# A two-layer graph transformer kernel: layer 0's unranked token tile becomes a block of its own, and the keys, list scatters and readback come in another order

## The chip, the cores and the metric

The kernel runs on one core of one Trainium2 chip. The metric is the device time of one execution in microseconds (us). Three runs of the kernel before took 1982.24, 1981.65 and 1976.04 us; their median is 1981.65 us. One more execution was profiled: it took 1979.62 us, of which 1977.7 us lie between its first and last instruction (the span). Unless another one is named, every time below is a time of that execution, counted from the start of its span.

## The reference

2708 tokens of width 512 pass through two layers of the same form. `adj` is a symmetric 0/1 matrix with ones on its diagonal; its rows are sparse (the longest has 20 entries). Cut to what matters, one layer is

```python
mask = adj.astype(float32) + eye(n)
q = (h @ Wq.T + bq).reshape(n, 8, 64)      # k and v likewise
scores = einsum('nhd,mhd->hnm', q, k) / sqrt(64)
scores = where(mask == 0, -1e9, scores)
attn = softmax(scores, axis=-1)
ctx = einsum('hnm,mhd->nhd', attn, v).reshape(n, 512)
h1 = layer_norm(h + ctx @ Wo.T + bo, ln1_g, ln1_b)
ff = relu(h1 @ W1.T + b1) @ W2.T + b2      # 512 -> 2048 -> 512
h2 = layer_norm(h1 + ff, ln2_g, ln2_b)
```

All of it is float32.

## The kernel before, in words

Work is tiled by 128 tokens: 21 full tiles and one of 20 tokens, 22 in all. Attention goes over the edges only. Each token has a list of its neighbours; the keys and values of a neighbour stand in one row of 1024 numbers of a table in HBM (`kv_d`), and an indirect DMA on POOL's queue (`gather`, L1063 on, recorded as L1065) fetches, for 128 tokens at once, one neighbour each (0.5 MB).

**Groups.** So that few gathers are wasted, tokens are sorted by the length of their lists into groups of 128. Group g has the static cap `CAPS[g]`: groups 0 to 19 fall from 22 to 5, group 20 (`FRESH`) has 18, the short group 21 has 3. Group FRESH isn't sorted: it is one token tile as it stands, number `STAR`, 18 before. Its lists are at hand as soon as the lists of all tiles are made; those of the other groups must first be scattered to their ranks in HBM (`rec_d`, 21 indirect DMAs, L800) and read back into the tile `new` (three DMAs, L814 and L822).

**Keys stage** (`first`). For each token tile PE projects k and v (8 matmuls of 128x512 each), DVE adds the bias to k (L908), ACT copies v (L911), and ACT's queue writes the rows to `kv_d`. Beside it `lists(t)` makes the lists: SP loads 1.35 MB of `adj` into one of two buffers (L679), POOL adds the diagonal (L680), ACT turns the row into codes (L684), DVE takes the largest of 11 segments (L687) and of those (L691, L694). `LEAD` = 1.3 lists are started for each key tile. The first key tiles were 20 and 21 (128 and 20 tokens, one block `XBS - 1` of x), then 0 to 19; x is loaded by SP in blocks of 256 columns, each behind lists already asked for. A tile of at most 32 tokens is projected in four quarters of the array (L571), and DVE adds three quarters afterwards (`plus_rest`, L586 for k and v).

**Query stage** (`first_queries`). PE projects q for the 22 tiles in the order of `tiles`, number j by j; DVE scales and adds the bias (L962, L973) and SP writes pairs of tiles to `q_d`. The first is STAR's. Between the tiles stand the steps of attention: `next(ahead)` and `advance(c)` go on with the generator `attend`, which asks for gathers some chunks ahead and computes one chunk (two slots of a list, `SLOTS` = 2) per step: `weights` (DVE, L1101 and L1107), one step later `weigh` (ACT exponentials and half of the products, L1120 and L1127; DVE the rest, L1133 and L1140), then `sums` (DVE, last L1163) and `divided` (ACT, tile `cx`, L1171). `moving` steps through `ranked`: 8 scatters at j = 2, two per j for j = 3 to 8, and at j = 9 the last one and the readback. `own_rows` fetches the x rows of the second group (19) at j = 11, `listed` turns the readback into indices at j = 17 and 18, `own_query` projects group 19's q at j = 19. At the last j `through(0)` runs attention until both groups of block 0 are done, and `attended` follows for each: PE turns cx (tp, L1255), projects with Wo (o, L576), DVE and POOL normalise (L1239 to L1249, POOL's L1245).

**Blocks.** The feed-forward part goes over blocks of two groups, w = 256 columns: for each of 16 slices f PE makes four matmuls pf (128x256, L1446), ACT applies bias and relu (ft, L1457), and three slices later PE adds one matmul of 128x512 for each group (a, L1419). Each logical f32 matmul is two records in the trace. Layer 0 has 11 blocks: (20, 19), (18, 17), (7, 9), ..., (21, 8). During block k, `through(k + 1)` at f = 10 (f = 11 in block 0) runs attention until the groups of the next block are done; the next slice projects them with Wo; at the last slice they are turned (`turned`). The keys and values of layer 1 of block k are made in block k + 1, f = 5 to 8. Between, each f steps attention by `PACE` (0.62 chunks in layer 0).

**What sets the order.** PE, ACT and SP run in the order of the program text. POOL does so until the end of block 0; DVE does in the query stage and until slice f = 5 of block 0 (`by_turns`), and elsewhere its order is a scheduler's. [...]

Of the kernel before, what the change touches and what calls it, by code (L numbers as in the profile page):

```python
# [18 lines left out]
P = 128  # L19
# [15 lines left out]
Q4 = 32  # L35

CAPS = (22, 14, 13, 12, 12, 11, 11, 10, 10, 9, 9, 9, 9, 8, 8, 8, 7, 7, 6, 5, 18, 3)
FRESH, STAR = 20, 18
SLOTS = 2
QB = 3  # L40
LAG = 3
# [3 lines left out]
XB, XBS = 256, 11  # L45
# [427 lines left out]
def by_edges(ctx: ExitStack, tc: tile.TileContext, x, xT, adj, layers, out, good):  # L473
# [9 lines left out]
    nc = tc.nc  # L483
# [366 lines left out]
    def first(w, meanwhile):  # L850

        nonlocal at
        xg = []
        stream = [XBS - 1] + list(range(XBS - 1))
        homes = [f"w{1 + i % 2}_{i // 2}" for i in range(XBS)]
        homes = homes[1:] + homes[:1]

        def load():
            i = len(xg)
# [34 lines left out]
        counts = counted()  # L894
        done, before = 0, None
        by_turns = ExitStack()
        for i, t in enumerate([NT - 2, NT - 1] + list(range(NT - 2))):
            r = size(t)
            if i == NT - 2:
                by_turns.enter_context(tc.manual_schedule(engines={mybir.EngineType.DVE}))  # L900
                next(counts)
            xs = tokens(t)
            home = ("w2_5", "w2_6", "w2_7", "w1_6", "w1_7")[i % 5]
            kv = wts.tile([P, 2 * DM], F32, tag=home, name="kvs")
            k = project(xs, r, wk, "k")
            if i == 0:
                finish(turning)
            nc.vector.tensor_tensor(kv[:r, :DM], k[:r], bk[:r], ALU.add)  # L908
            plus_rest(kv[:r, :DM], k, r)
            v = project(xs, r, wv, "v", other=True)  # L910
            nc.scalar.copy(kv[:r, DM:], v[:r])  # L911
            plus_rest(kv[:r, DM:], v, r)
            if before:
                nc.scalar.dma_start(**before)
            before = dict(out=kv_d[0][t * P : t * P + r, :], in_=kv[:r])
            if i == 0:
                finish(load())
                finish(load())
            while done < min(NT, 1 + LEAD * i):
                lists(done)  # L920
# [14 lines left out]
    def first_queries(bq, wq, counts, ranked, listed, tables, tokens, meanwhile):  # L935
# [15 lines left out]
            return own[g]  # L951

        moving = None
        tiles = [STAR] + [t for b in range(STAR // 2, NT // 2) for t in (2 * b, 2 * b + 1)]
        tiles = [t for i, t in enumerate(tiles) if i == 0 or t != STAR]
        tiles += range(STAR // 2 * 2)
        for j, t in enumerate(tiles):
            r = size(t)
            q = project(tokens(t), r, wq, "q", other=j % 2 > 0)
            if j == 0:  # L960
                to = new_q(FRESH)
                nc.vector.scalar_tensor_tensor(to, q, DK**-0.5, bq, ALU.mult, ALU.add)  # L962
                nc.sync.dma_start(out=q_d[0][t * P : (t + 1) * P, :], in_=to)
                next(ahead)
            else:
                if not made or len(made[-1][0]) == 2:
# [6 lines left out]
                nc.vector.scalar_tensor_tensor(  # L973
                    qs[:r, i], q[:r], DK**-0.5, bq[:r], ALU.mult, ALU.add
                )
                plus_rest(qs[:r, i], q, r, DK**-0.5)
            if j == 2:
                moving = ranked(*counts)
                for _ in range(8):
                    next(moving)  # L980
            if j > 2:
                advance(0.75)
                if j < 9:
                    for _ in range(2):
                        next(moving, None)
                elif above is None:
                    finish(moving)
                    tables.__exit__(None, None, None)
                    above = ctx.enter_context(
                        tc.tile_pool(name="above", bufs=1, side="right", reuse_waits="tile")  # L990
                    )
            if j == 11:
                xr = own_rows(order[1])
            if j == 17:
                listed(True)
                all_listed.append(True)
                advance(1.5)
            if j == 18:
                listed(False)
# [529 lines left out]
    NB = len(blocks)  # L1529
    orders = [[g for block in blocks for g in block] for blocks in plans]  # L1530
    blocks, order = plans[0], orders[0]

    def attend(n, got):
# [6 lines left out]
        for g in order:  # L1540
            cuts = chunks_of(g)
            steps += [(g, s0, c, i, i + 1 == len(cuts)) for i, (_, s0, c) in enumerate(cuts)]
            if g == order[1] or (n == 0 and g == order[0]):
                steps += [None] * 3
            if n == 0 and g == order[0]:
                steps.append("more")
# [71 lines left out]
    def beside_queries(j):  # L1618
# [14 lines left out]
    def both(a, b):  # L1633
        hs = []
        for part in (a, b):
            *_, h = part
            hs += h
        yield hs

    def temp():  # L1640
        return dn.tile([P, DM], F32, tag="h", name="temp", bufs=4)
# [6 lines left out]
    early[0] = list(early[0])  # L1648
    behind, pool = None, []
    for n in range(NL):  # L1650
        blocks, order = plans[n], orders[n]
        last = n == NL - 1
        nxt = None if last else Layer(n + 1, layers[n + 1])
        if n > 0:
# [24 lines left out]
        for k, block in enumerate(blocks):  # L1679
# [4 lines left out]
            for f, zs in enumerate(now.feed_forward(block, hs, hT)):  # L1684
                if f == NFC:
                    break
                if f == 5:
                    by_turns.close()
                if f in (5, 6, 7, 8) and behind:
                    next(behind)  # L1690
# [4 lines left out]
                if more and f == 11 + (k + n == 0):  # L1695
# [122 lines left out]
```

## Time and profile before

| what | us |
|---|---|
| median of three runs | 1981.65 |
| the profiled execution | 1979.62 |
| its span | 1977.7 |
| PE busy | 1858.0 |
| DVE busy | 1363.1 |
| ACT busy | 960.4 |
| POOL busy | 829.6 |

The span's 40 slices, with the busy share in tenths, show where PE isn't filled: mostly in the first eight slices (49.4 us each), which hold the keys, the queries and block 0. The prediction shows the lines. In the timelines each row is: start, duration, engine, line, operation, output<-inputs, shapes, count, and in brackets the idle time before it with what ended it. A count of 8 pf records is one slice f.

### The profile page before, as it was taken

The numbers are of one execution on the slowest core, as the hardware profiler recorded it, in microseconds if no ns is written. First come the engines' busy times: TensorE is split into PE (matmuls) and PEld (weight loads), VectorE is DVE, ScalarE is ACT, GpSimd is POOL, SyncE is SP. The second block draws the span as 40 slices with busy tenths as digits, with TensorE's granted clock in tenths as the row PEclk, the third lists the DMA queues.
The fourth block names the chain that finished last, engine by engine and source line by source line (L and its number), as shares of the span: only waits on it lengthen the run. The fifth ranks groups of instructions, "written<-read, shape, count | busy, mean of one in ns | idle before, by whom it ended". The sixth has DMA issues, their size and how long they took to land. (4 is left out here: it accounts for less than half of the span.)

```text
span 1977.7 us, 20995 instructions
## 1 busy us (share of the span) xinstructions
PE 1858.0 (94%) x6126; PEld 1094.8 (55%) x6126; DVE 1363.1 (69%) x2215; ACT 960.4 (49%) x3334; POOL 829.6 (42%) x732
## 2 busy tenths in 40 slices
PE   9799758899999999999999997999999999999997
PEld 3344325556566555655656553565566666666664
DVE  6886558758658686684840337586977999899522
ACT  3651226455537545474442213555465766666511
POOL 3114636535536455452410114353545765557101
PEclk9899979899999999999999999999999999999998
DMA  9995658556555565563411368565664776565000
GB/s 326 353 308 197 226 207 278 207 170 202 180 176 169 207 211 176 181 193 120 163 38 64 98 241 325 188 235 170 224 207 154 259 237 228 178 214 182 25 1 19
DMA packets 128751, 372.63 MB, mean 188 GB/s; under 512 B 17340, under 2 KB 31516, under 8 KB 125918
## 3 DMA queue, kind: packets, MB, share of 16 engines
q0 software_dynamic: 72176, 257.59, 39.2%
q1 hardware_dynamic: 45940, 92.02, 13.3%
q10 hardware_dynamic: 10510, 21.58, 3.0%
q8 instruction: 50, 0.82, 0.2%
q14 instruction: 75, 0.61, 0.1%
HBM read 320.33 MB, written 50.81 MB: 188 GB/s over the span
## 5 line engine op out<-in xcount | busy, mean ns | idle before, releaser
L1065 POOL DMA_INDIRECT kv<-kv_d,idx x442 | 569.8, 1289 | 486.3 <-DVE acc L1140 243.1
L1446 PE MATMUL pf<-hT,w 128*128 128x256 f32 (+1 forms) x2816 | 637.1, 374 | 7.2 <-ACT ft L1457 4.9
L1419 PE MATMUL a<-w,ft 128*128 128x512 f32 x1312 | 622.6, 600 | 12.5 <-ACT ft L1457 10.1
L1446 PEld LDWEIGHTS pf<-hT,w 128*128 128x128 f32 x2816 | 520.8, 191 | 182.6 <-issue 102.6
L1101 DVE TENSOR_TENSOR kv<-kv,q 128x1024 f32<-128x1024 f32 (+1 forms) x232 | 268.2, 1165 | 209.7 <-DMA kv<-kv_d,idx 171.8
L1419 PEld LDWEIGHTS a<-w,ft 128*128 128x128 f32 x1312 | 249.7, 193 | 209.4 <-issue 170.2
L1457 ACT ACTIVATE ft<-pf,b 128x256 f32<-128x256 f32 (+1 forms) x336 | 153.9, 463 | 416.8 <-PE pf L1446 413.7
L1127 ACT ACTIVATE kv<-kv,p 128x64 f32<-128x64 f32 x1328 | 335.2, 334 | 5.4
L1107 DVE TENSOR_REDUCE sc<-kv 128x16 f32<-128x1024 f32 (+1 forms) x232 | 267.2, 1160 | 1.6
L1140 DVE TENSOR_TENSOR acc<-acc,kv 128x1024 f32<-128x1024 f32 (+2 forms) x188 | 217.1, 1155 | 17.1 <-ACT kv L1127 13.9
L1245 POOL TENSOR_TENSOR rd<-va,mhalf 128x1 f32<-128x1 f32 (+1 forms) x88 | 91.1, 1035 | 286.9 <-DVE va L1243 285.9
L1120 ACT ACTIVATE p<-sc,minus 128x8 f32<-128x8 f32 (+1 forms) x442 | 108.1, 294 | 137.8 <-DVE sc L1107 115.1
L576 PE MATMUL o<-wo,cT 128*128 128x512 f32 x336 | 153.7, 610 | 12.0 <-ACT cT L1260 12.0
L1133 DVE TENSOR_TENSOR kv<-kv,p 128x512 f32<-128x512 f32 (+1 forms) x188 | 128.0, 681 | 24.1 <-ACT p L1120 24.1
L1171 ACT ACTIVATE cx<-acc,su 128x64 f32<-128x64 f32 (+1 forms) x352 | 88.5, 334 | 67.3 <-DVE su L1163 37.0
L576 PEld LDWEIGHTS o<-wo,cT 128*128 128x128 f32 x336 | 65.2, 196 | 95.7 <-issue 72.9
L684 ACT ACTIVATE code<-aj 128x2708 bf16<-128x2708 int32 (+1 forms) x22 | 71.0, 3227 | 50.3 <-POOL aj L680 48.5
L687 DVE MAX8 tops<-code 128x8 f32<-128x247 f32 (+2 forms) x242 | 84.0, 399 | 14.7 <-ACT code L684 14.5
L576 PE MATMUL k<-wk,xg 128*128 128x512 f32 x168 | 79.6, 618 | 15.2 <-DVE kvs L908 10.6
L1127 ACT ACTIVATE acc<-kv,p 128x64 f32<-128x64 f32 (+1 forms) x352 | 88.8, 334 | 1.5
L1028 POOL DMA_INDIRECT kv_d<-kvs,ident_i x22 | 24.5, 1114 | 154.9 <-ACT kvs L1506 94.8
L1249 DVE SCALAR_TENSOR_TENSOR h<-h,rd,ln_b 128x512 f32<-128x512 f32 (+1 forms) x88 | 65.6, 747 | 33.8 <-POOL rd L1245 33.8
(165 smaller groups left out, 1501.2 us busy)
## 6 DMA issues: line engine op xcount, KB each, us to landing
aj<-in_adj SPq DMA_DIRECT2D x21, 1354.0 KB
kv_d<-kvs ACTq DMA_DIRECT2D x21, 512.0 KB
w<-in_W ACTq DMA_DIRECT2D x16, 512.0 KB
w<-in_W SPq DMA_DIRECT2D x16, 512.0 KB
kv<-kv_d,idx POOLq DMA_INDIRECT x442
q_d<-qs SPq DMA_DIRECT2D x23, 256.0 KB
zT_d<-zT SPq DMA_DIRECT2D x22, 256.0 KB
xb_d<-h SPq DMA_DIRECT2D x21, 256.0 KB
```

The source lines that it names most:

```text
L576: nc.tensor.matmul(o[:r], xs(c), wm[:, c, :], start=(c == 0), stop=(c == NC - 1))
L1065: return nc.gpsimd.indirect_dma_start(out=to, out_offset=None, in_=table[:, :], in_offset=bass.IndirectOffsetOnAxis(ap=s, axis=0), bounds_ ...
L1101: nc.vector.tensor_tensor(kv[:r, :c, :DM], kv[:r, :c, :DM], self.q[:r].unsqueeze(1).to_broadcast([r, c, DM]), ALU.mult,)
L1107: nc.vector.tensor_reduce(self.sc[:r, s0 : s0 + c, :], kv[:r, :c, :DM].rearrange("p s (h d) -> p s h d", d=DK), AX.X, ALU.add,)
L1120: nc.scalar.activation(p[:r, s, :], self.sc[:r, s, :], AF.Exp, bias=minus[:r, g, s : s + 1])
L1127: nc.scalar.activation(to[:, i, hd], kv[:r, i, DM + h * DK : DM + (h + 1) * DK], AF.Copy, scale=p[:r, s0 + i, h : h + 1],)
L1133: nc.vector.tensor_tensor(to[:, 0, :].rearrange("p (h d) -> p h d", d=DK), kv[:r, 0, DM:].rearrange("p (h d) -> p h d", d=DK), p[:r, s0, : ...
L1140: nc.vector.tensor_tensor(self.acc[:r, :c, :], self.acc[:r, :c, :], kv[:r, :c, DM:], ALU.add)
L1245: nc.gpsimd.tensor_tensor(rd[:r], va[:r], mhalf[:r], ALU.pow)
L1419: nc.tensor.matmul(a[:r], fts[f][:, c0 : c0 + r], self.w2[f // 2][:, f % 2, :], start=(f == 0), stop=(f == NFC - 1),)
L1446: nc.tensor.matmul(pf[:, :w], self.w1[f // 2][:, c, f % 2 * P : f % 2 * P + P], hT[:, c, :w], start=(c == 0), stop=(c == NC - 1),)
L1457: nc.scalar.activation(ft[:, :w], pf[:, :w], AF.Relu, bias=self.b1[:, f : f + 1])
```

## The change

- `STAR` is 10 instead of 18: group FRESH is token tile 10. `CAPS` stays as it is.
- Layer 0 has 12 blocks: (20) alone, (19, 18), (17, 16), (7, 9), (6, 10), (5, 11), (0, 15), (1, 14), (2, 13), (3, 12), (4) alone, (21, 8). Layer 1's plan is the same as before.
- Keys come in the order 0 to 15, 20, 21, 16 to 19, and one block of x less is loaded at the start. Queries come in the order 10, 11, 0 to 9, 12 to 21.
- The scatters go 8 at j = 2, three per j for j = 3 to 6 and one at j = 7; the readback follows at j = 12, x rows of group 19 at j = 13.
- `through(0)`, which now asks for group FRESH alone, and its `attended` come at j = 19, ahead of group 19's query; tiles 20 and 21 are projected after it. `both` and the calls at the end of the query stage are gone.
- FRESH's x rows are fetched by a plain DMA on SP's queue instead of an indirect one on POOL's.
- In layer 0's block 0 attention steps by 0.5 chunks per slice instead of 1.1, `through(1)` comes at f = 13 instead of 11, and DVE keeps program order until f = 12 instead of 5.

```diff
-FRESH, STAR = 20, 18
+FRESH, STAR = 20, 10
...
-        stream = [XBS - 1] + list(range(XBS - 1))
-        homes = [f"w{1 + i % 2}_{i // 2}" for i in range(XBS)]
-        homes = homes[1:] + homes[:1]
+        stream = [*range(XBS - 3), XBS - 1, XBS - 3, XBS - 2]
+        asked = [STAR // 2] + [b for b in range(XBS) if b != STAR // 2]
+        homes = [f"w{1 + i % 2}_{i // 2}" for i in map(asked.index, stream)]
...
-        for i, t in enumerate([NT - 2, NT - 1] + list(range(NT - 2))):
+        for i, t in enumerate(t for b in stream for t in (2 * b, 2 * b + 1)):
...
             if i == 0:
                 finish(load())
-                finish(load())
...
-        tiles = [STAR] + [t for b in range(STAR // 2, NT // 2) for t in (2 * b, 2 * b + 1)]
-        tiles = [t for i, t in enumerate(tiles) if i == 0 or t != STAR]
-        tiles += range(STAR // 2 * 2)
+        tiles = [STAR, STAR ^ 1] + [t for t in range(NT) if t // 2 != STAR // 2]
...
-                if j < 9:
-                    for _ in range(2):
-                        next(moving, None)
-                elif above is None:
+                if j < 8:
+                    for _ in range(3 if j < 7 else 1):
+                        next(moving)
+                if j == 12:
                     finish(moving)
...
-            if j == 11:
+            if j == 13:
                 xr = own_rows(order[1])
...
             if j == 19:
+                through(0)
+                early[0] = list(now.attended(blocks[0], got))
                 zT = turned_own(order[1], xr)
...
-        if n == 0:
+        if n == 0 and g == FRESH:
+            nc.sync.dma_start(out=to, in_=table[STAR * P : (STAR + 1) * P, :])
+        elif n == 0:
             gather(to[:r], table, ident_i[:r, g : g + 1])
...
-    blocks = [(FRESH, 19), (18, 17), (7, 9), (6, 10), (5, 11), (0, 16)]
-    blocks += [(1, 15), (2, 14), (3, 13), (4, 12), (NT - 1, 8)]
+    blocks = [(FRESH,), (19, 18), (17, 16), (7, 9), (6, 10), (5, 11), (0, 15)]
+    blocks += [(1, 14), (2, 13), (3, 12), (4,), (NT - 1, 8)]
...
-        if j == NT - 2:
-            advance(1.0)
-        if j == NT - 1:
-            through(0)
-            early[0] = both(*(now.attended((g,), got) for g in blocks[0]))
...
-                if f == 5:
+                if f == 12:
                     by_turns.close()
...
-                if more and f == 10 + (k + n == 0):
+                if more and f == 10 + 3 * (k + n == 0):
                     through(k + 1)
...
-                advance(PACE[n] if k else 1.1 if f < 11 else 0.4)
+                advance(PACE[n] if k else (0.5, 1.1)[n] if f < 11 else 0.4)
```

More of the change, by code (lines that the diff above doesn't have):

```diff
@@ L965, in first_queries @@
             else:
-                if not made or len(made[-1][0]) == 2:
+                if j < 3 or len(made[-1][0]) == 2:
                     if len(made) > 1:
@@ L1528, in by_edges @@
     plans.append(blocks)
-    NB = len(blocks)
     orders = [[g for block in blocks for g in block] for blocks in plans]
@@ L1542, in attend @@
             steps += [(g, s0, c, i, i + 1 == len(cuts)) for i, (_, s0, c) in enumerate(cuts)]
-            if g == order[1] or (n == 0 and g == order[0]):
+            if g == order[1 + (n == 0)] or (n == 0 and g == order[0]):
                 steps += [None] * 3
@@ L1626, in beside_queries @@
             now.load_w2(len(now.w2), nc.scalar)
-        if j == NT - 2:
-            advance(1.0)
-        if j == NT - 1:
-            through(0)
-            early[0] = both(*(now.attended((g,), got) for g in blocks[0]))
[L1633 to L1638, printed above, removed]
     def temp():
@@ L1647, in by_edges @@
     first_queries(*made, beside_queries)
-    early[0] = list(early[0])
     behind, pool = None, []
@@ L1651, in by_edges @@
         blocks, order = plans[n], orders[n]
+        NB = len(blocks)
         last = n == NL - 1
@@ L1686, in by_edges @@
                     break
-                if f == 5:
+                if f == 12:
                     by_turns.close()
                 if f in (5, 6, 7, 8) and behind:
-                    next(behind)
-                if more and f == 10 + (k + n == 0):
+                    next(behind, None)
+                if more and f == 10 + 3 * (k + n == 0):
                     through(k + 1)
@@ L1694, in by_edges @@
                     next(projecting)
-                if more and f == 11 + (k + n == 0):
+                if more and f == 11 + 3 * (k + n == 0):
                     for hs_next in projecting:
                         advance(0.5 if k else 0.0)
-                advance(PACE[n] if k else 1.1 if f < 11 else 0.4)
+                advance(PACE[n] if k else (0.5, 1.1)[n] if f < 11 else 0.4)
                 if f in (0, 3, 7, 9):
```

## The prediction

> **What bounds the kernel now.** I read the page's slices first, then the windows by stage, then PE's timeline in the stages with gaps, and last the timelines of the engines that end those gaps.
>
> ```profile
> PE   9799758899999999999999997999999999999997
> ...
> PEclk9899979899999999999999999999999999999998
> ```
>
> PE is the bound: full in nearly every slice, except the 2nd and the 5th to 8th.
>
> ```profile
> 0.00:167.30 167.30, 152.11 (x368) 67.38 (x369) 128.55 (x454) 81.89 (x44) 25.85 (x65) 0.97 0.87 307
> 167.30:222.00 54.70, 54.67 (x137) 24.18 (x135) 35.24 (x60) 13.14 (x51) 38.72 (x34) 1.00 0.71 239
> 222.00:300.00 78.00, 41.37 (x93) 18.18 (x93) 46.15 (x70) 23.40 (x92) 28.47 (x30) 0.77 0.58 198
> 300.00:380.60 80.60, 68.61 (x219) 43.37 (x220) 62.24 (x82) 44.86 (x172) 48.12 (x37) 0.90 0.75 256
> 380.60:1130.00 749.40, 732.38 (x2487) 447.30 (x2486) 483.55 (x687) 369.71 (x1366) 309.03 (x254) 0.99 0.47 156
> ```
>
> Each row: window, its length, busy PE, PEld, DVE, ACT, POOL, then PE's clock, DMA share, GB/s. PE idles 15.2 us in the keys, 36.6 from 222 to 300, 12.0 in block 0 (300 to 380.6); the next 749 us lose 17. PE's gaps:
>
> ```profile
> 69.14 5.67 PE L576 MATMUL k<-wk,xg 128*128 128x512 f32 x8 [10.56 <-DVE kvs L908]
> ...
> 248.29 1.11 PE L1255 MATMUL tp<-ident,xr 128*128 128x128 f32 x4 [8.04 <-DVE qs L973]
> 254.82 6.69 PE L576 MATMUL q<-wq,zT 128*128 128x512 f32 x8 [5.42 <-ACT zT L1257]
> ...
> 279.88 6.11 PE L576 MATMUL o<-wo,cT 128*128 128x512 f32 x8 [11.06 <-ACT cT L1260]
> ...
> 298.40 1.11 PE L1255 MATMUL tp<-ident,h 128*128 128x128 f32 x4 [7.22 <-DVE h L1249]
> ```
>
> The 11.06 is the wait for group 19's attention, the 7.22 for its normalisation. Behind them stand POOL and DVE:
>
> ```profile
> 232.89 0.86 POOL L814 DMA_DIRECT2D new<-rec_d  x1 [5.44 <-DMA rec_d<-rec,ranks]
> ...
> 236.10 1.08 POOL L1065 DMA_INDIRECT kv<-kv_d,idx  x1 [0.16 <-DVE acc L1140]
> ...
> 297.75 1.53 POOL L1065 DMA_INDIRECT q<-q_d,ident_i  x1 [0.19 <-issue]
> ```
>
> FRESH's last two gathers (236.10) stand behind the readback, which waits for every scatter; group 18's query (297.75) stands behind the two POOL steps of block 0's normalisation. So DVE takes up 18 only at 302.51, and ACT finishes its cx at 326.8:
>
> ```profile
> 302.51 1.23 DVE L1101 TENSOR_TENSOR kv<-kv,q 128x1024 f32<-128x1024 f32 x1 [4.17 <-DMA q<-q_d,ident_i]
> ```
>
> ```profile
> 325.03 1.77 ACT L1171 ACTIVATE cx<-acc,su 128x64 f32<-128x64 f32 x7
> ```
>
> **What the skill says.** "TensorE: Matmul & The Clock Gate", Part 1 (HAM clock gate): after an idle window of about 3.4 us PE runs at half clock. The trace agrees: 8 q records took 6.69 us after the gaps, 3.43 when warm. The same page, LDWEIGHTS: a load takes P/1.2 ns for P columns, 107 ns for 128, as long as a 128-column matmul. Here L563 (128x128, f32) advances 8 records in 0.89 us, 111 ns each, so narrow blocks aren't load-bound. "DMA: Bandwidth & Descriptors", Anatomy of one DMA (SWDGE): 2.0 us plus bytes over 436 GB/s, 3.2 us for a gather. Here the pair issued by 199.55 let DVE start at 205.15: 5.6 us. I use 5.7.
>
> **Part 1, the key order.** At 58.6 PE stops until k of key tile number 6 is evacuated (68.41), because DVE's order puts that behind 8 lists. The changed instruction order, which can be read without a run, puts it behind 7 (61.9). With a full tile second instead of 20 tokens, PE gets there 6.9 - 1.8 = 5.1 us later. So this stall goes: 10.6 and 2.1 of slow clock. What is late next: the 20-token tile is now 18th, and DVE's adds on its k come behind the last list, whose MAX8 ended at 148.5; they release a PSUM buffer that the 21st k needs. The lists stay paced by the same DMA bytes (0.87 busy). DVE: 148.5 + 0.7 for the moved evacuation + two adds 1.4 = about 150.9, then two tiles of 6.9: keys end at 164.7, not 167.3. **-2.6**; both ends: -12.7 (lists early) to 0. One x block less ahead costs nothing: each still lands behind a list asked some 10 us before use; without that cover a tile waits about 6. All later times below are on the old clock; I subtract the 2.6 at the end.
>
> **Part 2, scatters and readback.** FRESH stays at 18 slots, since its cap stays (longest list 18 in tile 18, 16 in tile 10, counted from the inputs): shorter lists are worth nothing. POOL still issues 18 gathers and 21 scatters at 1.3 each. Three scatters per j instead of two only push single pairs back: pair 4 goes out by 201.1 (199.55 before), pair 6 by 218.6 (214.1). All FRESH gathers now precede the readback (5.44 of waiting, 3 of issuing). Pair 9 needs pair 5's buffer, which DVE frees one chunk late, at 228.6: it is issued by 231 and lands at 236.6, where before DVE got it at 243.23. A chunk costs DVE 1.2 + 1.2 + 0.7 + 1.2; between chunks 8 and 9 and the sums stand four qs evacuations (0.68 each): sums at 248.9 (252.25 before), cx 2.0 later at 251.0 (254.3). The readback, issued at 231 and landed some 3 later, is ready before its index step, which moves from 253.3 to 250.2. So FRESH gains 3.3 us and 19's gathers about as much.
>
> **Part 3, FRESH alone ahead of 19.** A q needs the PSUM buffer of the q six before, and DVE frees it between chunks: PE waits 5 us for j = 16 and is through with j = 19 at 243.3. It idles 8 until cx at 251.0, then tp, cT on ACT (1.1), and o with a cold clock (6.1, as at 279.88, where 3.43 is warm), done at 258.7; then 19's turn (0.6), its copy and query, and the tiles 20 and 21: free at 268.7. FRESH's normalisation lies beside these: DVE 258.7 to 265, with POOL's rd queued behind seven gathers of 19 and 18 (250.7 to 259.8), all inside PE's time. Before, nothing lay beside the 7.22. The new wait in `through(0)` queues 19's query and q of 20 and 21 behind it on PE; POOL's q gather of 18 waits for the last of these. hT stands on ACT behind 19's first two chunks (DVE 268.3 to 273.1, ACT 2.5 each, then hT 1.1): 277. **The feed-forward starts at 277, not 300.0.** The plain x fetch on SP saves POOL 1.3 off the path; it stands behind q writes done by 246, in time for o.
>
> **Part 4, block 0 of 128 columns.** A slice is 0.89 + 0.86 = 1.75 us; f = 13 would be reached at about 300. It needs cx of 19 and 18, and 18's query gather waits for all q_d writes: the last qs leaves DVE at 276.6; no row shows how soon a small write lands, so I take 2.4 (an estimate from the DMA page's 2.0; ends 1.5 and 5); the gather's issue and landing take 4.8 (297.75 to 302.51). DVE starts 18 at 284. Before, 24.3 us passed from there to cx (302.51 to 326.8), with chunks of 17 between; the new order again runs 17's four chunks ahead of 18's sums and has 19's last chunk and sums in it too (2 us): cx(18) at 310. `advance` by 0.5 and DVE's program order to f = 12 set that order; their price is in it. ACT holds ft of f = 8 behind that cx, and pf has three PSUM buffers, so PE stands at f = 11 from 296 for some 14 us. Then three slices 5.3, tp 0.9, a slice 1.75, two o 6.9 and 2.6 for the cold clock (279.88's 6.11 against 3.43): 327.5. 18's normalisation (4.5, with two chunk steps of 17 and a POOL wait between: 8.5), tp 0.9 and hT 1.1: block 1 starts at **338**.
>
> Compare at equal work. By 380.56 before had also run 17's tp, o, tp (4.3) and 19's feed-forward (8 x 3.44 = 27.5): 338 + 31.8 = 369.8. **-10.8**.
>
> **Part 5, the twelfth block.** Matmuls of two narrow blocks: 128 records each x (111 - 108) ns, 0.4 us each (block 0's is inside its slices); one boundary more, ends of 0.2 to 2 us in the timeline: **+1.0**. In (4) the attention for (21, 8), up to 7 chunks of 4.2 us DVE, lies beside slices and 14.6 us of keys; uncovered it would cost up to 8. From block 1 on PE has 72 us or more per wide block and DVE about 55: I leave the rest, and layer 1, unchanged.
>
> **Sum.** -2.6 - 10.8 + 1.0 = -12.4: 1979.62 to 1967.2 for the profiled execution, which is 2.0 below the median: 1981.65 - 12.4 = **1969**.
>
> **Rivals.**
> - The forecast, chance 0.50, 1962 to 1975.
> - *The covers hold* (0.20): the lists arrive early enough that the keys end 12.7 earlier, and 18's attention comes about 6 sooner. For: DVE is busy 46 of the 78 us from 222 to 300. Against: DVE is in order here, and the list pace is DMA's. -12.4 - 10 - 6: 1953.
> - *The wait only moves* (0.15): cx(18) comes 10 us later than I count (kv buffers, DMA at 0.75 of its time). -2.4: 1979, within 0.3% (about what a measurement of this kernel can tell from no change).
> - *Slower* (0.15): the readback at j = 12 starves the narrow block. Place: 18's gathers and query on POOL behind the readback; cx(18) no earlier than before (326.8) with half the feed-forward to cover it. Then block 0 ends 16.8 later, at 354.8, 386.6 at equal work: +6.0, keys 0, +1.0: 1989. It decides from cx(18) at 310 + 9.8, about 320. Against: POOL issues them in 25 us from 250.
> - That the change doesn't do what it says: true of the shorter lists, counted at nothing above.
>
> **Numbers.** Faster by over 0.3% (below 1975.7): forecast and first rival, 0.70. Within: 0.15. Slower: 0.15. Range 1952 to 1986: it leaves out under half of the first rival and most of the slower case; the likeliest's own is 1962 to 1975.
>
> **What would show it.** Right: the keys' 10.56 gap gone, a gap of about 9 near 135 to 150 instead; pf starting near 274; PE waiting in block 0 for ft with cx(18) near 307, then for h; pf 128x128 at 111 ns; block 1 near 335. Wrong: 18's cx beyond 317, narrow slices above 1.9 us without waits, or new gaps after block 1.

## The result, and the profile after

The changed kernel is slower: 1990.32 us, the median of five runs (1985.25 to 1992.28), against 1978.33 (1975.07 to 1982.24) for the kernel before on the same chip. The ratio is 1.0054 (95% interval 1.0033 to 1.0076). A second series gave 1.0048 (1.0030 to 1.0067). The forecast was 1969, range 1952 to 1986: faster, and the kernel became slower.

The profiled execution took 1985.25 us, with a span of 1983.4. It was the quickest of its five, as the second profile (1982.82) was of its nine. The medians differ by 12.0 us in the first series and by 10.5 in the second; the traces place 5.7 of that (1983.4 - 1977.7), and the rest stands in no trace. (The four slower executions of the first series show a mean granted clock of PE of 0.971 to 0.973, the profiled one 0.976.) All times below are from the start of the span.

The same view by stage as for the kernel before, cut where the stages of the changed kernel end (window, length, busy PE, PEld, DVE, ACT, POOL, PE's clock, DMA share, GB/s):

```profile
0.00:167.30 167.30, 154.53 (x368) 67.98 (x369) 129.28 (x454) 81.72 (x44) 25.79 (x65) 0.98 0.87 307
167.30:222.00 54.70, 54.70 (x133) 24.98 (x132) 31.26 (x55) 13.14 (x51) 38.72 (x34) 1.00 0.65 221
222.00:274.40 52.40, 34.10 (x82) 14.18 (x80) 40.08 (x56) 18.96 (x75) 22.47 (x25) 0.89 0.84 288
274.40:345.10 70.70, 45.41 (x192) 30.65 (x193) 43.12 (x63) 26.27 (x103) 27.32 (x26) 0.82 0.66 226
345.10:423.20 78.10, 73.26 (x253) 45.47 (x252) 56.66 (x78) 45.53 (x173) 38.13 (x33) 1.00 0.57 183
423.20:1125.00 701.80, 681.05 (x2337) 416.04 (x2336) 453.80 (x643) 346.82 (x1286) 299.20 (x235) 0.99 0.47 153
```

The third window idles 18.3 us where before idled 36.6. The fourth, block 0 with one group, idles 25.3 where before's idled 12.0 with two. Of the 18.3 us less of idling ahead of the feed-forward, block 0 takes back 13.3. PE's timeline shows the gaps:

```profile
135.49 5.40 PE L576 MATMUL v<-wv,xg 128*128 128x512 f32 x8 [2.71 <-ACT kvs L911]
151.81 5.40 PE L576 MATMUL k<-wk,xg 128*128 128x512 f32 x8 [4.05 <-DVE kvs L586]
...
274.46 6.21 PE L1447 MATMUL pf<-hT,w 128*128 128x128 f32 x32 [6.86 <-ACT hT L1261]
...
290.27 2.07 PE L1447 MATMUL pf<-hT,w 128*128 128x128 f32 x8 [5.24 <-ACT ft L1458]
...
313.32 2.08 PE L1447 MATMUL pf<-hT,w 128*128 128x128 f32 x8 [11.90 <-ACT ft L1458]
...
339.91 1.12 PE L1256 MATMUL tp<-ident,h 128*128 128x128 f32 x4 [7.60 <-DVE h L1250]
```

```profile
311.00 0.35 ACT L1172 ACTIVATE cx<-acc,su 128x64 f32<-128x64 f32 x1 [12.22 <-DVE su L1164]
```

The 10.56 us gap of the keys is gone and smaller ones have come late in the stage, as foretold. But the first q matmul comes at 167.34 in both kernels. In block 0, PE stands for ft, which on ACT is behind cx of 18 (the last row), and then for h of 18. Now both kernels at equal work (31.8 us is the prediction's price of what before has done more by block 1; by (21, 8) the changed kernel has made k and v of one tile more, 6.9 + 0.4):

| point | before | after | difference at equal work |
|---|---|---|---|
| keys end | 167.34 | 167.34 | 0 |
| feed-forward starts | 299.97 | 274.46 | |
| block 1 starts | 382.97 | 345.14 | -6.0 |
| block (21, 8) starts | 1114.01 | 1125.02 | +3.7 |
| layer 1's feed-forward starts | 1257.90 | 1262.75 | +4.9 |
| end of span | 1977.7 | 1983.4 | +5.7 |

So by block 1 the change had gained 6.0, and the blocks from there to (21, 8) lost 9.7. PE's waits between block 1 and (21, 8), first of the kernel before, then after (total us, times, longest):

```profile
PE tp L1255 <- DVE h L1249: 6.5, 2, 4.7
PE a L1419 <- ACT ft L1457: 6.1, 4, 2.3
PE tp L1255 <- ACT cx L1171: 3.8, 1, 3.8
PE pf L1446 <- ACT hT L1260: 0.2, 1, 0.2
```

```profile
PE tp L1256 <- DVE h L1250: 13.0, 4, 4.8
PE a L1420 <- ACT ft L1458: 6.5, 3, 2.7
PE tp L1256 <- ACT cx L1172: 5.1, 2, 3.7
```

24.6 us in all against 16.6: 8.0 of the 9.7 are such waits, and 6.5 of these 8.0 are for the normalised h of the next block. The longest, 4.78 us at 911.81, can be read on the engines that made it. First DVE, then POOL:

```profile
888.04 1.23 DVE L1102 TENSOR_TENSOR kv<-kv,q 128x1024 f32<-128x1024 f32 x1 [12.41 <-DMA kv<-kv_d,idx]
...
896.52 0.68 DVE L1385 TENSOR_TENSOR h<-o,xb 128x512 f32<-128x512 f32 x1
...
907.39 0.15 DVE L1244 TENSOR_SCALAR va<-mv 128x1 f32<-128x1 f32 x1
...
911.01 0.75 DVE L1250 SCALAR_TENSOR_TENSOR h<-h,rd,ln_b 128x512 f32<-128x512 f32 x1 [1.68 <-POOL rd L1246]
```

```profile
907.98 1.08 POOL L1066 DMA_INDIRECT kv<-kv_d,idx  x1 [0.30 <-issue]
909.37 0.99 POOL L1066 DMA_INDIRECT kv<-kv_d,idx  x1 [0.30 <-issue]
910.38 0.60 POOL L1246 TENSOR_TENSOR rd<-va,mhalf 128x1 f32<-128x1 f32 x1
```

DVE stands 12.4 us for a gather, then has a heap of chunk steps; these stand between the steps of h. The rd of the second group, 0.6 us of work, waits on POOL behind gathers: DVE has written its input va at 907.54, and two more gathers are issued first. The Trainium skill says of these engines ("PSUM — Partial Sum Buffer", Engine vs sequencer instructions) that their queues are strictly first in, first out. This trace agrees: rd starts at 910.38, when the issue ahead of it has ended (910.36). So DVE is busy only 65 to 73% of these blocks, and PE waits for it all the same.

### The profile page after: what moved, and what is told of

Same layout as the page of the kernel before. It is cut to its first block, busy times and chain, and to the rows that moved or that the text cites. A ratio compares the mean times of both kernels' runs of the same rounds, so it can differ in the third digit from the quotient of the medians.

```text
span 1983.4 us, 21276 instructions
## 1 busy us (share of the span) xinstructions
PE 1862.9 (94%) x6254; PEld 1102.0 (56%) x6254; DVE 1364.1 (69%) x2215; ACT 963.0 (49%) x3350; POOL 834.0 (42%) x731
## 5 line engine op out<-in xcount | busy, mean ns | idle before, releaser
L1447 PE MATMUL pf<-hT,w 128*128 128x256 f32 (+2 forms) x2944 | 640.2, 365 | 26.1 <-ACT ft L1458 17.1
L1447 PEld LDWEIGHTS pf<-hT,w 128*128 128x128 f32 x2944 | 530.9, 193 | 203.8 <-issue 112.0
L1458 ACT ACTIVATE ft<-pf,b 128x256 f32<-128x256 f32 (+2 forms) x352 | 157.3, 454 | 416.6 <-PE pf L1447 411.0
L687 DVE MAX8 tops<-code 128x8 f32<-128x247 f32 (+2 forms) x242 | 83.1, 401 | 18.2 <-ACT code L684 18.1
L576 PE MATMUL k<-wk,xg 128*128 128x512 f32 x168 | 80.0, 621 | 10.1 <-DMA wk<-in_Wk 4.8
```

Source lines behind the costliest of these rows:

```text
L576: nc.tensor.matmul(o[:r], xs(c), wm[:, c, :], start=(c == 0), stop=(c == NC - 1))
L1447: nc.tensor.matmul(pf[:, :w], self.w1[f // 2][:, c, f % 2 * P : f % 2 * P + P], hT[:, c, :w], start=(c == 0), stop=(c == NC - 1),)
L1458: nc.scalar.activation(ft[:, :w], pf[:, :w], AF.Relu, bias=self.b1[:, f : f + 1])
```

## The experiments

Seventeen runs followed, the first of them of the changed kernel again. Ratios are to the kernel before in the same series; 0.001 is 2 us.

**The base again** (no edit).

> The changed kernel once more, unedited, beside the three edits of this series and with a second profile: the base from which they are measured. Theory A (the profile of the changed kernel caught one of its quicker executions, with keys that ended at 167.3 where the same key order in four other kernels ended at 168.0 to 169.4): 1987 to 1991 us, keys end near 168.5, block 1 starts near 346. Rival (the first series was itself slow): 1983 or less.

1987.18 us, ratio 1.0048 (1.0030 to 1.0067). Keys end at 167.98, the feed-forward starts at 274.71, block 1 at 345.11, (21, 8) at 1128.13. Theory A holds for the time; of the slower keys only 0.6 us showed.

**The key order alone**, in the kernel before (the places of the x blocks follow it), and undone in the best kernel.

```diff
-        stream = [XBS - 1] + list(range(XBS - 1))
+        stream = [*range(XBS - 3), XBS - 1, XBS - 3, XBS - 2]
...
-        for i, t in enumerate([NT - 2, NT - 1] + list(range(NT - 2))):
+        for i, t in enumerate(t for b in stream for t in (2 * b, 2 * b + 1)):
...
-                finish(load())
                 finish(load())
```

> The kernel before with the new key order and the shorter load of x alone. Theory A (the stall of 10.6 us only moves, since DVE's lists and their DMA set the pace): the gap at 58 to 69 us goes, smaller ones come near 129 to 152, the first q matmul stays at 167.3 within 1 us, and the time is that of the kernel before within 2 us. Rival, my prediction's part 1: keys end 2.6 us earlier and the time falls by about 2.6. Second rival: the new key order itself carries part of the loss, and the time rises by 4 us or more.

1978.28 us, 1.0010 (0.9992 to 1.0027); keys end at 168.03.

> q_xb_cap with the keys in the order of the kernel before and its larger load of x: the key order undone alone, in a kernel where the stage after it has less slack. Theory A (the new order gains nothing): within 2 us of q_xb_cap's 1959.4. Rival, the prediction's -2.6: slower by 2.6 or more.

1959.29 us, 0.9906 (0.9890 to 0.9921), where the same kernel with the new order has 0.9912. So the key order is worth nothing either way. Over all traces, keys end between 165.1 and 168.0 in five kernels with the old order and between 165.7 and 170.3 in fourteen with the new one: in the mean 1.7 us later.

**FRESH's turn behind the queries of tiles 20 and 21.**

```diff
-            if j == 19:
+            if j == 21:
+                while made:
+                    written()
                 through(0)
```

> The changed kernel, but attention through FRESH, its output projection and group 19's query come at the last j (21) instead of j = 19, so that the queries of tiles 20 and 21 and their writes to q_d lie ahead of that wait. Theory A (18's query gather waits for the last q_d writes, and DVE waits 6.8 us for it): PE fills part of its 10 us wait for cx with 4.3 us of q, the q_d writes are out some 9 us earlier, DVE starts 18 at about 277 instead of 284.9, block 1 starts 5 to 8 us earlier than the changed kernel's 345.1, and the time falls by as much, to about 1983. Rival (the evacuations of these two q on DVE push cx of FRESH back, and DVE is then the bound up to cx of 18): within 2 us of the changed kernel, about 1990.

1975.97 us, 0.9996 (0.9982 to 1.0011): 10 us under the changed kernel (the profile, 1981.08, is of the slowest of its 14 executions). Block 1 starts at 339.31, 170.6 after the end of the keys (177.8 in the changed kernel), but not for the reason given: the feed-forward still starts at 274.43, because a new wait took the place of the old. SP's queue, DVE and PE:

```profile
258.13 0.35 SPq L1061 DMA_DIRECT2D xb<-in_x  x1
```

```profile
268.25 0.69 DVE L1387 TENSOR_TENSOR h<-o,xb 128x512 f32<-128x512 f32 x1 [10.54 <-DMA xb<-in_x]
```

```profile
272.84 1.09 PE L1258 MATMUL tp<-ident,h 128*128 128x128 f32 x4 [10.82 <-DVE h L1252]
```

FRESH's x rows, a plain load of 256 KB, now stand on SP behind the last q_d writes and land 10.1 us after they are issued, in the middle of 19's gathers. Still DVE took up 18 at 283.93, 115.2 after the keys instead of 117.6.

**The same with these x rows asked for at j = 16.**

```diff
+            if j == 16:
+                sooner[FRESH] = dn.tile([P, DM], F32, tag="row", name="xb", bufs=3)
+                fetch(0, sooner[FRESH], x, FRESH)
...
+                if self.n == 0 and g in sooner:
+                    xb = sooner.pop(g)
```

> q_first with FRESH's x rows fetched on SP at j = 16, ahead of the last q_d writes. In q_first this load is issued at 258.1, behind those writes, lands at 268.2, and DVE, which runs in order, stands 10.5 us before FRESH's h. Theory A (this wait took back what q_first had won): h is added at about 258, the feed-forward starts at about 264 instead of 274.4, 19's and 18's chunks come some 8 to 10 us sooner, block 1 starts at about 330 instead of 339.3, and the time is 5 to 9 us below q_first's, about 1969. Rival (the blocks after it are paced by the attention of the later groups, and give it back): block 1 starts early all the same, but the time is within 2 us of q_first's 1976.

1966.28 us, 0.9947 (0.9926 to 0.9968). On PE:

```profile
266.56 3.94 PE L1456 MATMUL pf<-hT,w 128*128 128x128 f32 x32 [0.51 <-ACT hT L1267]
...
305.58 2.07 PE L1456 MATMUL pf<-hT,w 128*128 128x128 f32 x8 [12.00 <-ACT ft L1467]
```

The feed-forward starts 96.2 after the keys (105.7 in q_first, 107.1 in the changed kernel) and block 1 at 164.0 (170.6, 177.8). The wait for cx of 18 stays at 12 us; it only comes sooner. From block 1 to (21, 8) it takes 773.9 us, where the changed kernel takes 779.9 and 783.0; PE's waits for h there are 6.6 us in all. So the plan itself can run with waits as small as before's.

**The driven run of block 0 two slices earlier.**

```diff
-                if more and f == 10 + 3 * (k + n == 0):
+                if more and f == 10 + (k + n == 0):
...
-                if more and f == 11 + 3 * (k + n == 0):
+                if more and f == 11 + (k + n == 0):
```

> The changed kernel with one part undone: in block 0 attention is driven through 19 and 18 at f = 11 instead of 13, and their output projection follows at f = 12 instead of 14. Theory A (18's sums stand on DVE behind the chunks of 17, which the later place lets the scheduler put first): cx of 18 is written about 4 to 6 us earlier than 313.0, and block 1 starts 3 to 5 us earlier than 345.1; time about 1986. Rival (PE then has two slices, 3.5 us, less to put before the wait, and what cx gains is lost again): block 1 within 1.5 us of 345.1, time about 1990.

1987.68 us, 1.0068 (1.0042 to 1.0094). cx of 18 begins 144.0 after the keys (143.7 in the changed kernel), so theory A's reason is wrong. Block 1 starts at 339.46, 170.1 after the keys, 7.7 sooner, since two slices now lie beside the normalisation; and it is given back at the end of block 1:

```profile
336.39 0.66 PE L1256 MATMUL tp<-ident,h 128*128 128x128 f32 x4 [0.78 <-DVE h L1250]
...
415.31 1.12 PE L1256 MATMUL tp<-ident,h 128*128 128x128 f32 x4 [7.67 <-DVE h L1250]
419.84 1.11 PE L1256 MATMUL tp<-ident,h 128*128 128x128 f32 x4 [3.41 <-DVE h L1250]
```

The 7.60 us wait became one of 0.78, and 11 us of the same kind followed one block on, where the changed kernel waits 2.92: the wait moved.

**The shorter cap** that token tile 10 allows (its longest list has 16 entries), with the changed kernel, with q_first, with q_xb, and with the kernel before.

```diff
-CAPS = (22, 14, 13, 12, 12, 11, 11, 10, 10, 9, 9, 9, 9, 8, 8, 8, 7, 7, 6, 5, 18, 3)
+CAPS = (22, 14, 13, 12, 12, 11, 11, 10, 10, 9, 9, 9, 9, 8, 8, 8, 7, 7, 6, 5, 16, 3)
```

> The changed kernel with CAPS of group FRESH 16 instead of 18, which is what the shorter lists of token tile 10 allow: 8 chunks instead of 9 in both layers, two gathers of 0.5 MB less in each. Theory A (DVE's chain from FRESH's chunks through 19 and 18 sets when the first blocks can start): cx of FRESH comes about 4 us earlier, block 1 starts 4 us earlier than 345.1 and the time falls by 4, to about 1985. Rival (the 18th query gather waits for the q_d writes, whose place is set by PE, and a chunk of DVE is not on the path): below 1.5 us, about 1988.

1974.94 us, 0.9989 (0.9978 to 0.9999): 12 to 13 us under the changed kernel by the ratios, three times what was expected. In its trace the feed-forward starts 101.2 after the keys instead of 107.1, so 5.9 is in FRESH's chain. Another 7 lies in layer 1 (713.3 from its feed-forward to the end, against 720.7); q_cap has the same cap and 720.7 there, so that part isn't tied to the cap. The base again, with no edit, has 716.7.

> q_first (FRESH's turn after the queries of tiles 20 and 21) together with CAPS of group FRESH 16. Theory A (both lie on the chain to cx of 18): the two gains add, cx of FRESH no longer waits for DVE while PE still has q to do, and the time is about 1972, 4 below q_first's 1976. Rival (PE's q work of the last tiles now ends last, at 252): as q_first, 1976.

1968.91 us, 0.9956 (0.9941 to 0.9971), 8 under q_first. The x rows held it too: in its trace PE waits 9.57 us for h.

> q_xb with CAPS of FRESH 16. Theory A: the gain of the shorter cap (q_cap stood 7 us under q_first) adds to that of the earlier x rows: about 1962. Rival (once h no longer waits for x, PE's last queries end the stage and not FRESH's chunks): as q_xb.

1959.44 us, 0.9912 (0.9891 to 0.9933): the gains add, by 7 us. This version beats both kernels.

For the kernel before, `STAR` is 10 as well, and the x blocks' places in SBUF follow the new order of the queries:

```diff
-FRESH, STAR = 20, 18
+FRESH, STAR = 20, 10
...
-        homes = [f"w{1 + i % 2}_{i // 2}" for i in range(XBS)]
-        homes = homes[1:] + homes[:1]
+        asked = [b % XBS for b in range(STAR // 2, STAR // 2 + XBS)]
+        homes = [f"w{1 + i % 2}_{i // 2}" for i in map(asked.index, stream)]
```

> The kernel before with token tile 10 as group FRESH and its cap 16: shorter lists alone, without the new block plan, key order, scatters or readback; queries start at tile 10 and run on to 21, then 0 to 9. Theory A (one chunk less on DVE's chain to FRESH's cx is worth some 7 us, since the attention of 19 and 18 stands behind it): about 1970. Rival (in the plan of before, group 19's attention and the readback set the start of the feed-forward, and a chunk less of FRESH is hidden): 1976 to 1979. It also tells whether FRESH alone is needed for what the best version so far (0.9912) gains.

1968.41 us, 0.9945 (0.9928 to 0.9963). The shorter list, in the old plan and with the order of queries that goes with tile 10, is worth 11 us by the ratio; its feed-forward starts at 290.85 instead of 299.97. Theory A holds, and the block plan isn't needed for it. Tile 10 with the cap of 18 was not run in the old plan, so the share of the order of queries isn't known.

**A late narrow block, and the new pairs, each alone in the kernel before.** For the first, each layer also takes its own number of blocks.

```diff
-    blocks += [(1, 15), (2, 14), (3, 13), (4, 12), (NT - 1, 8)]
+    blocks += [(1, 15), (2, 14), (3, 13), (4,), (12,), (NT - 1, 8)]
```

> The kernel before with its tenth block (4, 12) of layer 0 split into the narrow blocks (4) and (12); nothing else. It measures a twelfth block by itself, late, where attention has a long lead. Theory A (the extra block is cheap: two narrow blocks' slower matmuls 0.8 us and one more boundary of 1 to 2 us): +1 to +3 us. Rival (a narrow block has too little PE time to cover DVE and ACT, and is where the changed kernel loses its 10 us after block 0): +6 to +10 us.

1982.49 us, 1.0033 (1.0021 to 1.0045): +6.5 us, between the two theories and far from the prediction's +1.0. Its longest wait is in (4). There cx of 12 is in time: PE turns it at 1061.26 without a wait. It is cx of group 8, due only one block later, that stands on ACT ahead of ft and waits for its sums (128x80, which is 10 slots of 8 heads; 7, the only other group with 10 slots, is long done):

```profile
1077.36 2.01 PE L1446 MATMUL pf<-hT,w 128*128 128x128 f32 x8 [5.06 <-ACT ft L1457]
```

```profile
1075.04 2.02 ACT L1171 ACTIVATE cx<-acc,su 128x64 f32<-128x64 f32 x8 [4.46 <-DVE su L1163]
```

The changed kernel has no such wait in its narrow block (4).

```diff
-    blocks = [(FRESH, 19), (18, 17), (7, 9), (6, 10), (5, 11), (0, 16)]
-    blocks += [(1, 15), (2, 14), (3, 13), (4, 12), (NT - 1, 8)]
+    blocks = [(FRESH, 19), (18, 17), (7, 9), (6, 10), (5, 11), (0, 15)]
+    blocks += [(1, 14), (2, 13), (3, 12), (4, 16), (NT - 1, 8)]
```

> The kernel before with the later pairs of the changed kernel and nothing else: (0, 15), (1, 14), (2, 13), (3, 12), (4, 16) in the place of (0, 16), (1, 15), (2, 14), (3, 13), (4, 12); 11 blocks, no second narrow one. Theory A (the new pairs bring attention, normalisation and slices into another phase, which is where the changed kernel loses some 7 us from (7, 9) on): the time rises by 4 to 8, to about 1982, with waits for h of 10 us or more between block 1 and (21, 8). Rival (the loss comes from the narrow first block, after which the wide blocks carry more attention, and the pairs are indifferent): within 2 us of the kernel before.

1980.31 us, 1.0016 (1.0003 to 1.0028): +3, between both again. In its trace waits for h are 8.8 us (6.5 before), but from block 1 to (21, 8) it takes 731.3 us, where the kernel before takes 731.0. (That profile, 1977.87, is of its second quickest execution of 14.)

**Both narrow blocks first.**

```diff
-    blocks = [(FRESH,), (19, 18), (17, 16), (7, 9), (6, 10), (5, 11), (0, 15)]
-    blocks += [(1, 14), (2, 13), (3, 12), (4,), (NT - 1, 8)]
+    blocks = [(FRESH,), (19,), (18, 17), (7, 9), (6, 10), (5, 11), (0, 16)]
+    blocks += [(1, 15), (2, 14), (3, 13), (4, 12), (NT - 1, 8)]
```

> The changed kernel with another plan for layer 0: (20), (19), (18, 17), then the pairs of the kernel before, so that the second narrow block comes at once instead of tenth. Theory A (the changed kernel's wide blocks (19, 18) to (3, 12) take 37 us more than their own PE work where the wide blocks of the kernel before take 30, because of which group's attention falls due in which block): block 0 no longer waits 11.9 us for cx of 18, the blocks from (7, 9) on lose as little as before, and the time is 5 to 9 us below the changed kernel's, about 1980 to 1984. Rival (attention cannot keep up with two narrow blocks in a row, 7 chunks of 4.2 us beside some 42 us of PE work in (19)): the wait comes back in the block (19) and the time stays at 1988 or rises.

1993.18 us, 1.0081 (1.0067 to 1.0096). The rival holds. The end of the block (19):

```profile
391.98 1.12 PE L1256 MATMUL tp<-ident,h 128*128 128x128 f32 x4 [8.79 <-DVE h L1250]
397.50 1.11 PE L1256 MATMUL tp<-ident,h 128*128 128x128 f32 x4 [4.41 <-DVE h L1250]
401.32 5.49 PE L1420 MATMUL a<-w,ft 128*128 128x512 f32 x6 [2.71 <-ACT ft L1458]
```

Block 0 of this kernel still waits 11.59 us for ft, though only 19 falls due in it. ACT shows why: attention has been stepped into 18 all the same, and its cx stands ahead of the ft of f = 8, though the next block doesn't need it.

```profile
313.21 0.35 ACT L1172 ACTIVATE cx<-acc,su 128x64 f32<-128x64 f32 x1 [12.66 <-DVE su L1164]
```

**The pace of attention, up and down.**

```diff
-PACE = (0.62, 0.72)
+PACE = (0.72, 0.72)
```

> The changed kernel with attention stepped by 0.72 chunks per slice instead of 0.62 in layer 0's blocks from the second on (11.5 instead of 9.9 per block, where the pairs (6, 10) to (3, 12) need 11 and (0, 15) needs 15). Theory A (the waits at the ends of the wide blocks come from chunks that are left to the forced run at f = 10 and push the normalisation of h back): the sum of PE's waits from block 1 to block (21, 8) falls from 24.5 us to below 18 and the time by 5 to 8, to about 1982. Rival (DVE is the limit there, or its order is the scheduler's anyway): within 2 us of the changed kernel, or slower, since steps come ahead of h.

2006.01 us, 1.0143 (1.0120 to 1.0166). The other way, with `PACE = (0.55, 0.72)`:

> The changed kernel with attention stepped by 0.55 chunks per slice instead of 0.62 in layer 0's blocks from the second on; at 0.72 it took some 17 us longer, so the lag theory fell. Theory A now (attention steps taken in the last slices of a block come on DVE and ACT ahead of the next block's normalisation and of ft, and PE waits for these): PE's waits from block 1 to (21, 8) fall below the changed kernel's 24.5 us and the time by 3 to 8, to about 1983. Rival (the forced run at f = 10 gets longer and PE waits for cx there): 1988 or more.

2008.15 us, 1.0155 (1.0130 to 1.0180). Both theories A fall: more steps per slice cost 18 us, fewer cost 21. PE's waits over the same blocks, at 0.72 and then at 0.55:

```profile
PE a L1420 <- ACT ft L1458: 18.7, 8, 6.1
PE tp L1256 <- DVE h L1250: 13.5, 3, 5.5
```

```profile
PE tp L1256 <- DVE h L1250: 23.0, 8, 7.0
PE tp L1256 <- ACT cx L1172: 11.9, 4, 6.7
```

The waits fit attention that stands before ft on ACT where it runs ahead, and before h on DVE, or is late as cx, where it lags; the chains behind them were not followed.

**The driven run of the wide blocks one slice earlier**, in the changed kernel and in q_xb_cap.

```diff
-                if more and f == 10 + 3 * (k + n == 0):
+                if more and f == 9 + n + 4 * (k + n == 0):
...
-                if more and f == 11 + 3 * (k + n == 0):
+                if more and f == 10 + n + 4 * (k + n == 0):
```

> The changed kernel with attention driven through the next block's groups at f = 9 instead of 10 and their output projection at f = 10 instead of 11, in layer 0's blocks from the second on. Theory A (the 9.7 us lost from block 1 to (21, 8) are waits at block ends for h and ft, because the normalisation has too few slices before the turn): one slice more, 3.4 us, takes most of these waits away, PE's waits there fall from 24.5 us below 17, and the time by 5 or more, to about 1982. Rival (cx is not ready a slice earlier, so the wait moves from h to cx): 1987 or more.

2005.09 us, 1.0140 (1.0125 to 1.0156).

```profile
PE tp L1256 <- ACT cx L1172: 15.9, 2, 12.2
PE a L1420 <- ACT ft L1458: 9.4, 8, 1.8
PE pf L1447 <- ACT hT L1261: 4.7, 2, 2.8
...
PE tp L1256 <- DVE h L1250: 0.2, 1, 0.2
```

The waits for h are gone (0.2 us), and those for cx, ft and hT are 18 us longer: the rival.

> q_xb_cap with the step of through_9. Theory A: as in the changed kernel, 5 us less, about 1954. Rival: 1959 or more.

1976.03 us, 0.9997 (0.9985 to 1.0009), 17 worse than q_xb_cap. The same.

**The same plan, block by block.** The time of each block of layer 0, from its first pf to that of the next block, in three traces with the same plan, pace and place of the driven runs, each of the quickest execution of its series:

| block | changed kernel | the base again | q_xb_cap |
|---|---|---|---|
| (19, 18) | 78.1 | 77.8 | 77.9 |
| (17, 16) | 80.5 | 80.5 | 80.4 |
| (7, 9) | 81.3 | 81.3 | 80.1 |
| (6, 10) | 78.4 | 79.2 | 78.4 |
| (5, 11) | 91.0 | 90.2 | 87.1 |
| (0, 15) | 79.7 | 84.4 | 83.2 |
| (1, 14) | 86.4 | 83.4 | 80.3 |
| (2, 13) | 81.3 | 83.0 | 79.4 |
| (3, 12) | 74.0 | 74.0 | 74.0 |
| (4) | 49.1 | 49.1 | 49.1 |
| all ten | 779.9 | 783.0 | 770.0 |

The kernel before took 731.0 over these blocks, which is 770.1 at equal work (31.8 + 7.3 more). So in q_xb_cap the new plan loses nothing there. And (4) takes 49.1 us in all thirteen traces with this plan: the loss lies in the wide blocks before it, and not in the late narrow one.

## Why the prediction was wrong, step by step

The forecast of -12.4 and the +5.7 of the traces lie 18.1 us apart: 2.6 in the keys, 4.8 by block 1, and 10.7 from there to the end.

- **Part 1, the key order: the place right, the size wrong.** The gap of 10.56 went and gaps came at 135 and 152, with k of 20 tokens released at 151.8 (forecast 150.9). The 8 records behind it then ran with a slow clock (5.40 us, where warm ones after a wait take 3.70). These 0.9 and 1.7 are the 2.6. keys_only and best_old_keys confirm 0 to +2.
- **Parts 2 and 3: right, with some luck.** The prediction kept the old clock up to its sum, and the keys did end at the old time, so its times are compared on that clock. cx of FRESH was done at 251.8 (251.0), and PE waited for cx and for hT, as forecast; but q held PE until 246.7 (243.3), so the wait for cx was 3.7 and not 8. The feed-forward started at 274.46, where the chain said 277: "near 274" had taken off 2.6 that the keys did not give, so that hit is luck. "Shorter lists are worth nothing" is right for the change as made, since the cap stays; with before_star 11 of the 17 us that the best kernel gained can be had in the old plan.
- **Part 4, block 0: -10.8 became -6.0.** DVE took up 18 at 284.91 (284), by two errors that hid each other. The last qs left DVE at 274.9 (276.6), but the gather of 18's query was issued 4.8 us later (2.4 taken, 5 as upper end; the 2.4 came from a figure for DMAs that POOL issues, and these go out on SP):

```profile
279.73 1.02 POOL L1066 DMA_INDIRECT q<-q_d,ident_i  x1 [4.55 <-DMA bk<-in_bk]
```

```profile
284.91 1.23 DVE L1102 TENSOR_TENSOR kv<-kv,q 128x1024 f32<-128x1024 f32 x1 [6.78 <-DMA q<-q_d,ident_i]
...
298.46 1.23 DVE L1102 TENSOR_TENSOR kv<-kv,q 128x1024 f32<-128x1024 f32 x1 [2.62 <-DMA q<-q_d,ident_i]
```

The label names a load that SP issued just after; that POOL waited for the q_d writes is read from the program, not from the label. The 298.46 is 17's first chunk, which waits for its own query ahead of 18's sums; cx of 18 was done at 313.0 (310). Block 1 came at 345.1, not 338. Of these 7.1 us, 2.4 were there at the end of o (330.0 for 327.5), 1.5 came with h of 18 (10.0 from the end of o instead of 8.5), and 3.2 are the `a` matmuls of three slices between the last tp and block 1, which the sum left out (4.3 with a cold clock, less the 1.1 of hT that they hide). The other way went 2.4: the sum compared with 380.56, which in the kernel before lies within these same `a` matmuls, while its block 1 starts at 382.97. q_first and then q_xb, which take the last queries and the x rows out of this chain, bring block 1 7 and 14 us sooner after the end of the keys.
- **Part 5: the step that failed.** "From block 1 on PE has 72 us or more per wide block and DVE about 55: I leave the rest, and layer 1, unchanged" put the waits inside the wide blocks at no change. The blocks from block 1 to (21, 8) lost 9.7 us, 8.0 of them in PE's waits for h, cx and ft (24.6 us, before 16.6), and 2 more were lost from there to the end. The +1.0 for the twelfth block is not what failed: none of these waits lies in (4). A mean of busy time over a block doesn't see that the steps of h stand among chunk steps on DVE and behind gathers on POOL; the wait at 911.81 shows this once. Why the wide blocks wait longer in this kernel is not shown. late_narrow (+6.5) and late_pairs (+3) add up to about the 9.7, but they don't explain it: the longest wait of the first isn't in the changed kernel, and the trace of the second loses almost nothing over these blocks (731.3 us against 731.0). Nor is it a fixed price of the plan, since q_xb_cap pays none of it.
- **The signs and the rivals.** "New gaps after block 1" was on the prediction's list of signs that it is wrong, and it is the one that came. The slower rival named 1989, but by luck: in it the readback holds cx of 18 back to 326.8 or later, and that cx came at 313.0. The keys didn't end 12.7 earlier, as *the covers hold* had it, and cx of 18 was 3 us late, not 10 as in *the wait only moves*.

What stays open: which alignment makes the changed kernel's waits for h 13.0 us when q_xb, with the same plan, pace and order of blocks, has 6.6. Two other paces and one other place of the driven run were tried, and each was worse. A slower step of attention in block 0, and taking rd off POOL's queue, were not run. And the 4 to 5 us between the profiled executions and the medians of the changed kernel lie in no trace.

## What to carry to other kernels

Where several engines work in order and in lockstep with the bound one, price a new block plan by what must end in the last slices of each block, not by busy shares. A narrow block has half the cover for the same chain, and that matters where attention has no lead: PE idled 25.3 us in block 0, while it waited for nothing in (4). Making a stage start earlier is worth what its last input gains: here the feed-forward started 25.5 us earlier, and block 1 6 at equal work. Look for work that can go (a cap of 16 for 18, with tile 10: 11 us in the kernel before), for a wait that holds work back which doesn't need it (10 us in q_first), and for loads that stand behind writes on one queue (10 us in q_xb).

## What was not expected of the hardware

- A plain load of 256 KB took 10.1 us from its issue (258.13, q_first) to its use, with seven gathers of 0.5 MB issued between 252.7 and 261.4. In the changed kernel the same load was issued at 246.81 and used at 257.82 without a wait for it, so that trace shows only that it took 11.0 us or less.
- PE's clock falls after shorter gaps than expected. "TensorE: Matmul & The Clock Gate", Part 1, of the Trainium skill gives an idle window of about 3.4 us. Here 8 records after a gap of 2.71 us took 5.40 instead of 3.70, at a granted clock of 0.67, and in keys_only after one of 1.94 (with another of 2.10 six us earlier) as well, while in q_first a gap of 2.64 was followed by 3.70. These gaps are shorter than the page's window, so page and traces differ here, and the measurement decides. The page also says that the window runs freely; that this is why like gaps end differently is not shown by any run.
